# Layer 1's edge sums of a two-layer graph network, taken by quarters of the nodes instead of whole groups

## The chip, the cores and the metric

The kernel runs on one core of one Trainium2 chip. The metric is the device time of one execution in microseconds (us); three runs of the kernel before took 2122.86, 2127.27 and 2133.31 us, so its time is the median, 2127.27 us.

The engines that matter here work side by side, each through its own instructions in order: TensorE (PE in the profile, with its weight loads as PEld), VectorE (DVE), ScalarE (ACT), GpSimd (POOL), and SyncE (SP), which only issues transfers. GpSimd also issues the gathers, transfers whose source rows come from a list of indices.

## The reference

There are 3125 nodes with 768 features, and 53125 directed edges, sorted by their target node `dst`. Each edge has one of three relations. Two layers of the same attention (the first with four heads of 192 columns, the second with one head of 768) are followed by a residual sum and a layer normalisation:

```python
def rgat_conv(x, W, q, k, b, src, dst, etype, heads, out_ch, n_nodes):
    xr = jnp.einsum('nd,rdf->rnf', x, W)          # 3 relations
    oi = xr[etype, dst]
    oj = xr[etype, src]
    alpha = jax.nn.leaky_relu(oi @ q + oj @ k, 0.2)
    m = jax.ops.segment_max(alpha, dst, num_segments=n_nodes)
    e = jnp.exp(alpha - m[dst])
    z = jax.ops.segment_sum(e, dst, num_segments=n_nodes)
    a = e / (z[dst] + EPS)
    msg = (a[:, :, None] * oj.reshape(-1, heads, out_ch)).reshape(-1, heads * out_ch)
    return jax.ops.segment_sum(msg, dst, num_segments=n_nodes) + b

h = jax.nn.elu(rgat_conv(x, W1, q1, k1, b1, src, dst, edge_type, 4, 192, n))
out = rgat_conv(h, W2, q2, k2, b2, src, dst, edge_type, 1, 768, n)
x = _layernorm(x + out)
```

What the change concerns is the last `segment_sum` of layer 1: for every node, the sum over its edges of the attention weight times the source's row.

## The kernel before

**Groups and slots.** The nodes are cut into 25 groups of up to 128. The edges of a group, which lie together because they are sorted, are read as 17 slots of 128 edges (14 for the first group), 422 slots in all. One edge of a slot sits on each of the 128 partitions.

**Three phases.** `phase1` multiplies the nodes by layer 1's weights, stores the rows in a table in memory, and works out every edge's attention weight `pall` (four heads). `phase2` gathers the edges' source rows, sums them per node (layer 1's output), applies bias and ELU, and multiplies by layer 2's weights. `phase3` does layer 2's attention and sums and the normalisation. In this text `phase2` is the middle stage and `phase3` the last.

**The middle stage, slot by slot.** Slot k goes through these steps:

- `gather(k)`: GpSimd gathers 128 rows of 772 numbers into `gs[k % 9]`, one of nine tiles named `share`.
- `high(k)`: ScalarE writes H, the row times the edge's weight (four instructions, one a head) rounded to the type fp32r; VectorE or, for two slots in three, GpSimd writes `sel`, a 128x128 matrix that is 1 where an edge (row) belongs to a node (column).
- `low(k)`: VectorE writes L, what that rounding lost (four instructions).
- `sums(k)`: TensorE multiplies `sel` with H and with L, two halves each, so four matmuls of 128x386, and adds them up in `acc` in PSUM over all slots of the group.

Four early slots (k = 1, 3, 5, 7; `whole`) go another way: VectorE writes the selection matrices with the weights already in them (four of 128x128), and TensorE multiplies them with the unrounded rows, in plain fp32, which the trace shows as two matmul records for every one in the code.

When a group's sums are complete, `e_y` divides by the sum of weights and adds the bias (VectorE), `e_x` is an exponential (ScalarE), `e_h` finishes the ELU (VectorE), `e_t` transposes the result with six matmuls (TensorE), `e_s` and `e_s2` split it into two fp32r parts, and 18 pieces `d_part` of six matmuls each multiply it by layer 2's weights. `d_row` copies their sums to a row tile and stores it.

**The order is written out by hand.** The loop at the end of `phase2` counts k. Iteration k issues `gather(k)`, `sums(k - LAG)`, `low(k - LAG + 2)`, `high(k - LAG + 3)` with LAG = 8, and the events of that iteration: one `d_part` of the previous group in nearly every iteration, and the `e_` steps of a finished group over five iterations. Each engine executes its share strictly in that order.

**The last stage sums otherwise.** Because a slot's edges are sorted by node, they fall into a window of one or two quarters (32 nodes) of the group. `WINDOW` lists the quarters of each of the 17 slots, 25 pairs of slot and quarter in all, and `ROUNDS` orders the slots in seven rounds; a round's slots lie in different quarters. In `phase3` the selection matrix (`selp`) has only 32 or 64 columns and holds the weight, and each matmul has 32 output rows: the program gives it one of four column strips of the array (the profile writes 128*32 in place of 128*128). A check, `windows`, sends inputs that don't fit to a slower kernel.

Of the kernel before, what the change touches and what calls it, by code (L numbers as in the profile page):

```python
# [8 lines left out]
F32 = mybir.dt.float32  # L9
F32R = mybir.dt.float32r  # L10
# [3 lines left out]
AF = mybir.ActivationFunctionType  # L14
ALU = mybir.AluOpType
# [5 lines left out]
P = 128  # L21
# [11 lines left out]
def _index(ap):  # L33
    return bass.IndirectOffsetOnAxis(ap=ap, axis=0)
# [3 lines left out]
SL = 17  # L38
# [7 lines left out]
WINDOW = ((0,), (0,), (0,), (0, 1), (0, 1), (1,), (1,), (1, 2), (1, 2), (1, 2), (2,), (2, 3), (2, 3), (2, 3),  # L46
          (3,), (3,), (3,))

ROUNDS = ((0, 7, 15), (1, 8, 16), (2, 9, 14), (3, 11), (4, 12), (5, 13), (6, 10))
# [3 lines left out]
def kernel(  # L53
# [21 lines left out]
    R = layers[0]["W"].shape[0]  # L75
    E = src.shape[0]
    NB = (N + P - 1) // P
# [3 lines left out]
    l1, l2 = layers  # L81
    H1 = l1["H"]
    F1 = D // H1
    EP = 125
    ET = E // EP
    assert EP * ET == E and D % P == 0 and H1 == 4 and l2["H"] == 1 and R == 3
    RW = D + 4
    HW = RW // 2
    CW = F1 + 1
    LL = FRONT + E + BACK  # L90
    NK = (NB - 1) * SL + SLF
    V, S, G, T = nc.vector, nc.scalar, nc.gpsimd, nc.tensor
# [8 lines left out]
    tab1 = dram.tile([NP * R, RW], F32, name="ftab1")  # L101
# [8 lines left out]
    row = keep.tile([P, P], F32, name="frow")  # L110
# [22 lines left out]
    dl = keep.tile([P, NB, SL + 1], F32, name="fdl")  # L133
    rel = keep.tile([P, NB, SL], F32, name="rel")
    pall = keep.tile([P, NB, SL, H1], F32, name="pall")
# [131 lines left out]
    def split_parts(work, pts, w, name="t"):  # L267

        parts = []
        for i, pt in enumerate(pts):  # L270
            H, L = (work.tile([P, 2, w if name != "t" else 2 * P], F32R, name=f"{name}{s}{i}",
                              bufs=2 if name == "t" else 1) for s in "HL")
            S.copy(H[:, :, :w], pt[:, :, :w])
            V.tensor_sub(L[:, :, :w], pt[:, :, :w], H[:, :, :w].bitcast(F32))
            parts.append((H, L))
        return parts
# [168 lines left out]
    def base(b):  # L445

        return SLF + (b - 1) * SL if b else 0

    def slots(b):
        return SL if b else SLF  # L450

    def slot(k):

        return divmod(k - SLF + SL, SL) if k >= SLF else (0, k)

    ends = {base(b) + slots(b) - 1 for b in range(NB)}
    regs = {}

    def gather_rows(to, tab, b, j):

        i = ridx[:, b]
        if b in first_rows:
            i = rfirst[:, first_rows[b]]
        return G.indirect_dma_start(out=to, out_offset=None, in_=tab, in_offset=_index(i[:, j:j + 1]),  # L464
                                    bounds_check=NP * R - 1, oob_is_err=False)
# [361 lines left out]
    def phase2(work, psum, wH, wL):  # L827
        bias1 = work.tile([P, D], F32, name="fbias1", bufs=1)
        nc.sync.dma_start(bias1, l1["b"][None, :].to_broadcast([P, D]))
        last_w2 = second_weights(R - 1, wH, wL)  # L830
        gs = share
        NG = len(gs)
        rows = [work.tile([P, RW], F32, name=f"r2_{i}", bufs=1) for i in range(3)]
        for t in rows:
# [2 lines left out]
        st = {}  # L837
        blk = {}
        order = range(NB)
        ends2 = ends  # L840

        def gather(k):
            b, j = slot(k)
            gather_rows(gs[k % NG], tab1, b, j)

        def whole(k):

            return k < 8 and k % 2 == 1

        def high(k):  # L850
            b, j = slot(k)
            g = gs[k % NG]
            if whole(k):
                sel = work.tile([P, H1, P], F32, name="L", bufs=3)
                for h in range(H1):
                    V.tensor_scalar(sel[:, h], row, dl[:, b, j:j + 1], pall[:, b, j, h:h + 1],
                                    op0=ALU.is_equal, op1=ALU.mult)
                st[k] = sel
                return
            H = work.tile([P, RW], F32R, name="H", bufs=4)  # L860
            for h in range(H1):
                c = slice(h * CW, (h + 1) * CW)
                S.activation(H[:, c], g[:, c], AF.Copy, scale=pall[:, b, j, h:h + 1])  # L863
            sel = work.tile([P, P], F32R, name="sel", bufs=4)
            (V if k % 3 == 0 else G).tensor_scalar(sel, row, dl[:, b, j:j + 1], None, op0=ALU.is_equal)  # L865
            st[k] = [sel, H]

        def low(k):
            if whole(k):
                return  # L870
            b, j = slot(k)
            g = gs[k % NG]
            H = st[k][1]
            L = work.tile([P, RW], F32R, name="L", bufs=3)
            for h in range(H1):
                c = slice(h * CW, (h + 1) * CW)
                V.scalar_tensor_tensor(L[:, c], g[:, c], pall[:, b, j, h:h + 1], H[:, c].bitcast(F32),  # L877
                                       op0=ALU.mult, op1=ALU.subtract)
            st[k].append(L)

        def sums(k):
            b, j = slot(k)
            if j == 0:
                blk[b] = {"acc": psum.tile([P, 2, 512], F32, name="acc", bufs=2)}
            acc = blk[b]["acc"]
            if whole(k):
                sel = st.pop(k)
                for h in range(H1):
                    c = slice(h % 2 * CW, (h % 2 + 1) * CW)
                    T.matmul(acc[:, h // 2, c], sel[:, h], gs[k % NG][:, h * CW:(h + 1) * CW], start=False,  # L890
                             stop=(k in ends2), skip_group_check=True)
                return
            sel, H, L = st.pop(k)
            for i, a in enumerate((H, L)):
                for c in range(2):
                    T.matmul(acc[:, c, :HW], sel, a[:, c * HW:(c + 1) * HW], start=(j == 0 and i == 0),  # L896
                             stop=(k in ends2 and i == 1), skip_group_check=True)

        def e_y(b):
            s = blk[b]  # L900
# [10 lines left out]
        def e_x(b):  # L911
            s = blk[b]
            s["ey"] = work.tile([P, D], F32, name="ey", bufs=1)
            S.activation(s["ey"], s["y"], AF.Exp)
# [57 lines left out]
        def when(k, f, *a):  # L972
            ev.setdefault(k, []).append((f, a))

        LAG = 8
        first = SLF + LAG - 1
        for d, f in ((0, e_h), (1, e_t), (1, e_s), (1, e_s2)):
            when(first + d, f, order[0])
        for i, b in enumerate(order):
            e = SLF + i * SL + LAG  # L980
            if i > 0:
                for d, f in ((0, e_y), (1, e_x), (2, e_h), (3, e_t), (4, e_s), (4, e_s2)):
                    when(e + d, f, b)
            e += 6
            for m in range(6 * R):
                rc = divmod(m // 3, 2)
                k = e + m * SL // (6 * R) if i else first + 2 + m * (SL + 6) // (6 * R)
                when(k, d_part, b, *rc, m % 3)
                if m % 3 == 2:
                    when(k + 1, d_row, b, *rc)  # L990
            when(e + 2 + SL, d_q, b)
        for k in range(max(ev) + 1):
            if k < NK:
                gather(k)
            if k in (14, 19, 23, 26, 28):
                next(last_w2, None)
            if 0 <= k - LAG < NK:
                sums(k - LAG)
            if k == first:
                e_y(order[0])  # L1000
                e_x(order[0])
            if 0 <= k - LAG + 2 < NK:
                low(k - LAG + 2)
            if 0 <= k - LAG + 3 < NK:
                high(k - LAG + 3)
            for f, a in ev.get(k, []):
                f(*a)
            if k == NK + LAG:
                for b in range(len(xbs)):
                    x_load3(b)  # L1010

    def x_load3(b):

        nc.sync.dma_start(xbs[b % len(xbs)], nodes(b, xb_d))


    def phase3(work, psum):
# [3 lines left out]
        NG = 44  # L1021
        gs = work.tile([P, NG, RW], F32, name="G", bufs=1)
# [4 lines left out]
        st = {}  # L1027
# [95 lines left out]
        def a_put(b):  # L1123
            s = blk[b]
            s["p"] = work.tile([P, SL], F32, name="p2", bufs=3)
            V.tensor_copy(s["p"], s["pa"][:, 3 * P:3 * P + SL])

        def rounds(b):
            return [[j for j in r if j < slots(b)] for r in ROUNDS]

        def high(b, n):

            for j in rounds(b)[n]:
                p = blk[b]["p"][:, j:j + 1]
                lo, hi = WINDOW[j][0] * 32, WINDOW[j][-1] * 32 + 32
                sel = work.tile([P, 64], F32, name="selp", bufs=10)[:, :hi - lo]
                V.tensor_scalar(sel, row_p[:, lo:hi], dl[:, b, j:j + 1], p, op0=ALU.is_equal, op1=ALU.mult)  # L1137
                st[b, j] = sel
# [93 lines left out]
        LAG = SL + 10  # L1232
        for b in range(NB):
# [7 lines left out]
            e = base(b) + slots(b)  # L1241
# [21 lines left out]
    with tc.manual_schedule():  # L1263
        with tc.tile_pool(name="share", bufs=1) as pool:
            share = [pool.tile([P, RW], F32, name=f"share{i}") for i in range(9)]
# [3 lines left out]
            with tc.tile_pool(name="wbuf", bufs=1) as wbuf:  # L1269
                wH = wbuf.tile([P, R * DT, D + 2], F32R, name="wH")  # L1270
                wL = wbuf.tile([P, R * DT, D + 2], F32R, name="wL")
                with tc.tile_pool(name="pre", bufs=1) as pre:
                    qq = pre.tile([P, NB, H1, R], F32, name="qq")
                    with tc.tile_pool(name="work0", bufs=1) as work, tc.tile_pool(
                        name="psum0", bufs=1, space=PSUM
# [20 lines left out]
                    with tc.tile_pool(name="work1", bufs=1) as work, tc.tile_pool(  # L1296
                        name="psum1", bufs=1, space=PSUM
# [544 lines left out]
```

## Time and profile before

The profiled execution took 2122.86 us, 4.4 us under the median of the runs; its span, from the first instruction to the last, is 2121.1 us.

| stretch of the span | us | PE busy | DVE busy | ACT busy | POOL busy | granted PE clock | DMA |
|---|---|---|---|---|---|---|---|
| phase 1 and before (0 to 700) | 700 | 627.8 | 346.9 | 165.9 | 485.9 | 0.94 to 0.98 | 54 to 65% |
| start of the middle stage (700 to 740) | 40 | 29.2 | 35.3 | 27.5 | 34.1 | 0.69 | 92% |
| middle stage (740 to 1490) | 750 | 742.9 | 724.5 | 662.1 | 652.7 | 1.00 | 79 to 80% |
| its end (1490 to 1560) | 70 | 44.7 | 26.8 | 11.0 | 23.5 | 0.79 | 64% |
| last stage (1560 to 2122) | 562 | 371.5 | 330.4 | 96.0 | 407.6 | 0.71 to 0.77 | 51 to 94% |

How such views are read: the busy time of a stretch says which engines could bound it; the groups of instructions give the number, the total busy time and the mean duration of one kind of instruction; the chain of work that ended last is followed back from the end, and names at each moment the instruction that everything later hung on; the timeline lists instructions in order with the time at which they start. A duration is not the distance to the next instruction of the same engine: matmuls and VectorE instructions overlap their neighbours, so the distance from start to start is what an instruction costs an engine that is never idle.

### The profile page before, as it was taken

The page shows a single profiled execution, that of the slowest core. Times are in us where ns is not written, and L with a number is a line of the kernel's source. Part 1 is how long each engine was busy: PE and PEld are TensorE (multiplying, and loading weights), DVE is VectorE, ACT ScalarE, POOL GpSimd, SP SyncE. Part 2 cuts the span into 40 slices and gives each one's busy share as a digit, 9 for nine tenths or more (in the row PEclk, how much of TensorE's full clock was granted, in tenths as well). Part 3 has the DMA queues.
Part 4 walks back from the last instruction along what each step waited for, and adds up shares of the span by engine and source line. Part 5 has one row for each costly group of instructions (what it writes and reads, how often), then busy time and mean ns, then how long its engine had stood idle before and what let it go on. Part 6 is the DMA issues. An engine that isn't in the chain of part 4 may idle for free.

```text
span 2121.1 us, 38492 instructions
## 1 busy us (share of the span) xinstructions
PE 1816.0 (86%) x11755; PEld 1614.9 (76%) x11755; DVE 1463.8 (69%) x4299; ACT 962.4 (45%) x2331; POOL 1603.8 (76%) x1604
## 2 busy tenths in 40 slices
PE   6979998999979699999999999999856676676774
PEld 5979988999979599999999999999823343443433
DVE  6545544545543799999999999999456656656654
ACT  5411211122211588888888888888201211111111
POOL 5257777777777888888888888888177777777773
PEclk9999999999999799999999999999967777777787
DMA  6555544455538887777888778878499999999993
GB/s 184 188 146 171 194 159 148 158 187 171 171 115 266 279 260 246 232 242 242 259 247 251 246 246 251 249 244 249 162 311 325 329 338 336 328 329 317 317 321 131
DMA packets 156843, 506.10 MB, mean 239 GB/s; under 512 B 43875, under 2 KB 57069, under 8 KB 156628
## 3 DMA queue, kind: packets, MB, share of 16 engines
q0 software_dynamic: 81904, 331.52, 49.5%
q1 hardware_dynamic: 64494, 156.04, 21.2%
q10 hardware_dynamic: 10230, 15.98, 2.2%
q8 instruction: 97, 1.59, 0.3%
q14 instruction: 118, 0.97, 0.1%
HBM read 412.55 MB, written 95.69 MB: 240 GB/s over the span
## 4 chain that ended last, share of the span: by engine, by line
PE 61%; issue 11%; POOL 11%; DVE 8%; DMA 7%; ACT 1%; POOLq 0%; SPq 0%; ACTq 0%; DVEq 0%
PE po L951 21%; PE acc L896 13%; PE acc L1151 11%; POOL kt L464 8%; PE po L700 8%; DMA G<-ftab,ridx 2%; POOL G L464 2%; DMA kt<-kt,ridx 1%; PE bank L285 1%; PE pt L263 1%; DVE L L877 1%; DVE F L1108 1%; PE pt L926 1%; PE bc L1055 1%; PE po L399 1%
## 5 line engine op out<-in xcount | busy, mean ns | idle before, releaser
L863 ACT ACTIVATE H<-share,pall 128x193 fp32r<-128x193 f32 x1672 | 619.4, 447 | 83.5 <-PE acc L896 43.2
L877 DVE SCALAR_TENSOR_TENSOR L<-share,pall,H 128x193 fp32r<-128x193 f32 x1672 | 622.3, 437 | 19.9 <-issue 13.0
L951 PE MATMUL po<-wH,hT 128*128 128x386 f32 (+1 forms) x1800 | 529.7, 339 | 0.2 <-DVE hT L939 0.2
L464 POOL DMA_INDIRECT share<-ftab,ridx x374 | 421.2, 1126 | 80.5 <-DVE L L877 33.6
L464 POOL DMA_INDIRECT kt<-kt,ridx x374 | 395.0, 1056 | 114.6 <-issue 109.4
L464 POOL DMA_INDIRECT G<-ftab,ridx x374 | 379.8, 1015 | 114.0 <-issue 84.7
L700 PE MATMUL po<-wH,xT 128*128 128x384 f32 x1584 | 440.6, 348 | 10.1 <-ACT share L715 4.4
L951 PEld LDWEIGHTS po<-wH,hT 128*128 128x128 f32 x1800 | 334.4, 189 | 0.7 <-DVE hT L939 0.5
L700 PEld LDWEIGHTS po<-wH,xT 128*128 128x128 f32 x1584 | 294.0, 191 | 16.7 <-ACT share L715 6.3
L951 PE MATMUL po<-wL,hT 128*128 128x386 f32 (+1 forms) x900 | 304.9, 339 | 0.0
L1151 PE MATMUL acc<-G,selp 128*32 128x386 f32 x2488 | 299.3, 578 | 3.6 <-DVE selp L1137 2.1
L700 PE MATMUL po<-wL,xT 128*128 128x384 f32 x792 | 270.0, 341 | 0.0
L1151 PEld LDWEIGHTS acc<-G,selp 128*32 128x32 f32 x2488 | 185.9, 127 | 79.6 <-issue 46.6
L896 PE MATMUL acc<-H,sel 128*128 128x386 f32 x836 | 223.8, 349 | 10.8 <-POOL sel L865 9.7
L865 POOL TENSOR_SCALAR sel<-frow,fdl 128x128 fp32r<-128x128 f32 x278 | 215.9, 777 | 15.4 <-PE acc L896 4.7
L896 PE MATMUL acc<-L,sel 128*128 128x386 f32 x836 | 218.3, 343 | 0.0
L715 ACT COPY share<-po 128x384 f32<-128x384 f32 x144 | 67.7, 477 | 276.3 <-PE po L700 273.0
L1202 ACT ACT_TABLE_LOAD x24 | 30.8, 1283 | 356.2 <-DVE sd L1198 356.2
L951 PEld LDWEIGHTS po<-wL,hT 128*128 128x128 f32 x900 | 169.7, 189 | 0.0
L896 PEld LDWEIGHTS acc<-H,sel 128*128 128x128 f32 x836 | 150.8, 190 | 17.5 <-POOL sel L865 15.8
L896 PEld LDWEIGHTS acc<-L,sel 128*128 128x128 f32 x836 | 155.4, 192 | 0.2 <-DVE L L877 0.2
L1061 DVE TENSOR_SCALAR sT<-bc,cols 128x512 bf16<-128x512 f32 (+1 forms) x125 | 83.4, 667 | 99.0 <-PE bc L1055 98.9
(248 smaller groups left out, 2140.9 us busy)
## 6 DMA issues: line engine op xcount, KB each, us to landing
ftab<-share SPq DMA_DIRECT2D x75, 386.0 KB
ftab<-r SPq DMA_DIRECT2D x75, 386.0 KB
share<-in_L_gnn_W_dram SPq DMA_DIRECT2D x36, 384.0 KB
w_d<-w2hl SPq DMA_DIRECT2D x18, 768.0 KB
sT<-dr_d SPq DMA_DIRECT2D x25, 544.0 KB
share<-in_x_dram SPq DMA_DIRECT2D x25, 384.0 KB
xb_d<-share SPq DMA_DIRECT2D x25, 384.0 KB
xr<-in_x_dram SPq DMA_DIRECT2D x23, 384.0 KB
```

Of the source, the lines that this page charges most:

```text
L263: T.transpose(pt[:, f, c * P:(c + 1) * P], a[:, (2 * i + f) * P:(2 * i + f + 1) * P], ident)
L464: return G.indirect_dma_start(out=to, out_offset=None, in_=tab, in_offset=_index(i[:, j:j + 1]), bounds_check=NP * R - 1, oob_is_err=False)
L700: m = T.matmul(po[:, :HALF], xT[:, s, t, :], w[:, i, sl], start=(n == 0), stop=(n == 3 * DT - 1))
L715: S.copy(to, po[:, :HALF].rearrange("p (h f) -> p h f", h=2))
L863: S.activation(H[:, c], g[:, c], AF.Copy, scale=pall[:, b, j, h:h + 1])
L865: (V if k % 3 == 0 else G).tensor_scalar(sel, row, dl[:, b, j:j + 1], None, op0=ALU.is_equal)
L877: V.scalar_tensor_tensor(L[:, c], g[:, c], pall[:, b, j, h:h + 1], H[:, c].bitcast(F32), op0=ALU.mult, op1=ALU.subtract)
L896: T.matmul(acc[:, c, :HW], sel, a[:, c * HW:(c + 1) * HW], start=(j == 0 and i == 0), stop=(k in ends2 and i == 1), skip_group_check=True)
L951: T.matmul(po[:, :wd], hT[:, k, t, :], w[:, r * DT + t, sl], start=(t == 0 and n == 0), stop=(t == DT - 1 and n == 2))
L1061: V.tensor_scalar(s["sT"][:, 4 * i * P:4 * i * P + n], bc[:, :n], cols[:, b:b + 1], None, op0=ALU.is_equal)
L1151: T.matmul(acc[32 * t:32 * t + 32, c, :HW], st[b, j][:, 32 * (t - WINDOW[j][0]):][:, :32], gs[:, (base(b) + j) % NG, c * HW:(c + 1) * HW], ...
L1202: S.activation(sd, sd, AF.Sqrt)
```

## The change

In the middle stage, H, L, the 128x128 `sel` and the `whole` path go. VectorE writes, for each slot, four selection matrices with the weights in them (one a head), 32 or 64 columns wide, 9 slots deep. TensorE multiplies them in plain fp32 with the gathered rows, a quarter and a head at a time (32 output rows, 193 columns). The slots of a group are taken in the order of `ROUNDS` (`in_turn`), and the sums are issued two rounds at a time: after the sixth, the eleventh, the fifteenth and the last slot of a group (four batches). The ring of gathered rows grows from 9 tiles to 14. LAG is 5 in place of 8, and the steps of the first group move a little. The function `rounds` moves out of `phase3`; the last stage is otherwise the same, instruction for instruction.

```diff
-        gs = share
+        gs = share + [work.tile([P, RW], F32, name=f"g{i}", bufs=1) for i in range(5)]
...
+        def in_turn(k):
+            b, i = slot(k)
+            return b, [j for r in rounds(b) for j in r][i]
 
         def gather(k):
-            b, j = slot(k)
-            gather_rows(gs[k % NG], tab1, b, j)
+            gather_rows(gs[k % NG], tab1, *in_turn(k))
...
         def high(k):
-            H = work.tile([P, RW], F32R, name="H", bufs=4)
-            for h in range(H1):
-                c = slice(h * CW, (h + 1) * CW)
-                S.activation(H[:, c], g[:, c], AF.Copy, scale=pall[:, b, j, h:h + 1])
-            sel = work.tile([P, P], F32R, name="sel", bufs=4)
-            (V if k % 3 == 0 else G).tensor_scalar(sel, row, dl[:, b, j:j + 1], None, op0=ALU.is_equal)
+            b, j = in_turn(k)
+            lo, hi = WINDOW[j][0] * 32, WINDOW[j][-1] * 32 + 32
+            sel = work.tile([P, H1, 64], F32, name="selp", bufs=9)
+            for h in range(H1):
+                V.tensor_scalar(sel[:, h, :hi - lo], row[:, lo:hi], dl[:, b, j:j + 1], pall[:, b, j, h:h + 1],
+                                op0=ALU.is_equal, op1=ALU.mult)
+            st[b, j] = sel, gs[k % NG]
...
-        def low(k):
-                V.scalar_tensor_tensor(L[:, c], g[:, c], pall[:, b, j, h:h + 1], H[:, c].bitcast(F32),
-                                       op0=ALU.mult, op1=ALU.subtract)
...
         def sums(k):
-            for i, a in enumerate((H, L)):
-                for c in range(2):
-                    T.matmul(acc[:, c, :HW], sel, a[:, c * HW:(c + 1) * HW], ...)
+            b, j = in_turn(k)
+            n = [i for i, r in enumerate(rounds(b)) if r[-1] == j]
+            if not n or n[0] % 2 == 0 and n[0] < len(ROUNDS) - 1:
+                return
...
+            o = [(i, t) for r in rounds(b) for i in r for t in WINDOW[i]]
+            for m, h in ((m, h) for m in range(n[0] // 2 * 2, n[0] + 1) for h in range(H1)):
+                c = slice(h % 2 * CW, (h % 2 + 1) * CW)
+                for i, t in o:
+                    if i not in rounds(b)[m]:
+                        continue
+                    u = [x for x, y in o if y == t]
+                    sel, g = st[b, i]
+                    T.matmul(acc[32 * t:32 * t + 32, h // 2, c], sel[:, h, 32 * (t - WINDOW[i][0]):][:, :32],
+                             g[:, h * CW:(h + 1) * CW], start=(i == u[0] and h % 2 == 0), stop=(i == u[-1]),
+                             skip_group_check=True)
...
-        LAG = 8
+        LAG = 5
         first = SLF + LAG - 1
-        for d, f in ((0, e_h), (1, e_t), (1, e_s), (1, e_s2)):
+        for d, f in ((0, e_h), (3, e_t), (3, e_s), (3, e_s2)):
             when(first + d, f, order[0])
...
-                low(k - LAG + 2)
-            if 0 <= k - LAG + 3 < NK:
-                high(k - LAG + 3)
+                high(k - LAG + 2)
```

## The prediction

> **What bounds the kernel now.** The change lies in the middle stage only, so I first read the busy times by stretch, then the chain of waits inside the stage, then the groups of its instructions, and last the timeline of the last stage, which already sums in the new way.
>
> Two stretches, the middle stage and the last (columns: length; PE, PEld, DVE, ACT, POOL busy with counts; granted clock, DMA share, GB/s):
>
> ```profile
> 1000.00:1250.00 250.00, 249.42 (x1425) 248.02 (x1424) 242.83 (x713) 222.26 (x597) 217.53 (x225) 1.00 0.80 248
> 1800.00:2050.00 250.00, 168.26 (x1391) 97.96 (x1390) 152.95 (x452) 45.44 (x57) 192.40 (x190) 0.76 0.92 322
> ```
>
> TensorE is busy for 249.4 of 250 us at full clock in the middle stage; VectorE, at 97%, is close behind, so taking work from VectorE, ScalarE or GpSimd alone gains little. The chain of waits there (start us, us, what) is TensorE and next to nothing else:
>
> ```profile
> 1003.08 2.13 PE po L951 x12
> 1005.21 0.71 PE acc L896 x4
> 1005.92 1.06 PE po L951 x6
> ```
>
> A slot's sums (L896, four matmuls) cost TensorE 0.71 us, a piece of the product with the second layer's weights (L951, six) 1.06 us. The first term is what changes. In the groups (count, then busy us, mean ns) the other engines' share of it, and the last stage's `selp`:
>
> ```profile
> L863 ACT ACTIVATE H<-share,pall 128x193 fp32r<-128x193 f32 x1672 | 619.4, 447 | 83.5 <-PE acc L896 43.2
> L877 DVE SCALAR_TENSOR_TENSOR L<-share,pall,H 128x193 fp32r<-128x193 f32 x1672 | 622.3, 437 | 19.9 <-issue 13.0
> L1137 DVE TENSOR_SCALAR selp<-row_p,fdl,p 128x32 f32<-128x32 f32 x222 | 65.4, 304 | 42.8 <-PE acc L1151 41.9
> L1137 DVE TENSOR_SCALAR selp<-row_p,fdl,p 128x64 f32<-128x64 f32 x200 | 63.3, 337 | 5.5 <-PE acc L1151 5.5
> L865 POOL TENSOR_SCALAR sel<-frow,fdl 128x128 fp32r<-128x128 f32 x278 | 215.9, 777 | 15.4 <-PE acc L896 4.7
> ```
>
> And the new kind of sum, in the last stage's timeline (start us, us), with its durations (min/median/max ns) below:
>
> ```profile
> 1703.91 0.39 PE L1055 MATMUL bc<-d,one 1*128 1x512 bf16 x1
> 1704.23 2.80 PE L1151 MATMUL acc<-G,selp 128*32 128x386 f32 x28
> 1704.58 0.13 PEld L1151 LDWEIGHTS acc<-G,selp 128*32 128x32 f32 x4 [0.19 <-issue]
> 1704.90 0.13 PEld L1151 LDWEIGHTS acc<-G,selp 128*32 128x32 f32 x4 [0.20 <-issue]
> 1706.96 0.39 PE L1055 MATMUL bc<-d,one 1*128 1x512 bf16 x1
> 1708.70 1.01 POOL L464 DMA_INDIRECT G<-ftab,ridx  x1 [0.30 <-issue]
> 1710.02 1.01 POOL L464 DMA_INDIRECT G<-ftab,ridx  x1 [0.30 <-issue]
> ```
>
> ```profile
> L1151 PE MATMUL acc<-G,selp x2488: 484/488/856, 1560.4 to 2107.1; 128*32 128x386 f32 x192
> ```
>
> The same view of the start of the middle stage: selections and fp32 sums of the `whole` path, the first group's last sum, the first product piece; below, from the chain there, a gather that lands late:
>
> ```profile
> 711.08 1.11 DVE L856 TENSOR_SCALAR L<-frow,fdl,pall 128x128 f32<-128x128 f32 x4
> 714.80 1.48 PE L890 MATMUL acc<-share,L 128*128 128x193 f32 x8
> 728.33 0.85 PE L896 MATMUL acc<-L,sel 128*128 128x386 f32 x2
> 734.63 0.40 PE L951 MATMUL po<-wH,hT 128*128 128x386 f32 x1
> ```
>
> ```profile
> 713.40 8.60 DMA share<-ftab,rfirst
> ```
>
> The weight loads come four at a time, 0.325 us apart (1704.58, 1704.90): up to four quarters' matmuls start together, and the next four after 0.325 us. A start of four thus costs what one 386-column fp32 record costs. For 193 columns L890 gives it: eight in 1.48 us, the last of which takes 0.33, so (1.48 - 0.33) / 7 = 0.165 us from start to start, half of 0.325, with 128 weight columns loaded behind each.
>
> **The sums on TensorE.** Removed: 17 x 0.71 = 12.07 us a group. Added: seven rounds x four heads x two records = 56 starts of up to four, 56 x 0.165 = 9.24 us a group. The L1151 count confirms two records a matmul (2488 for 1244 in the code).
>
> The Trainium skill's page TensorE: Matmul & The Clock Gate, section "Part 3: Packing small matmuls", speaks against this: four packed row tiles gave 3.07 times the speed there, three column tiles 2.38. By that page a group's sums would take an estimated 9.24 x 4 / 3.07 = 12.0 us, and nothing would be saved. The row here has four starting in the time of one, so 9.24 stays.
>
> **The switch between whole and quarter matmuls.** Each of the four batches a group stands between L951 pieces, so TensorE changes shape 8 times a group. The trace prices it at L1055, a whole-width matmul among quarters. A 386-column fp32 record takes 0.488 and is followed after 0.325, so 0.163 of a duration is tail; L1055 (0.39) should be followed after 0.22, and is after 0.315 (1703.91 to 1704.225): 0.09 in. The last quarters start at 1704.23 + 2.80 - 0.49 = 1706.54, the whole one at 1706.96, after 0.42 in place of 0.325: 0.10 out. The second start of a batch comes 0.02 late, and the first 128-column weight load after it isn't hidden: 0.10, what a sums' first matmul loses after a wait in the middle stage (two in 0.62 us against 0.52). Together 0.31 a batch. Ends: 0.20 (the two drains alone) and 0.70 (each switch waits for the whole tail, 0.163, and a 128-column load, 0.19). I take 0.31, the nearest row.
>
> The Trainium skill's page TensorEngine Tiling (Array Packing), section "Key Properties", says that a change of the tiling mode drains the engine. It names no price; the trace agrees that there is one, 0.09 to 0.10 a switch.
>
> **After the first product piece.** Before, from 734.63 to the stage's last matmul at 1527.5, 407 slots' sums stand on the chain: 407 x 0.71 = 289.0 us. After: 24 groups x 9.24 = 221.8, and 96 batches x 0.31 = 29.8. The gain is 37.4 us. The 450 pieces (477 us) and 25 transposes stay.
>
> **What covers the rest, and what if not.** VectorE loses L877 (a group's 68) and gets 68 `selp`: 36 of 32 columns, 32 of 64. At L1137's mean durations, 36 x 0.304 + 32 x 0.337 = 21.7 us, plus some 6 for a group's other VectorE work (four `y` 1.6, `e_h` 1.5, the hT part 0.95, ten small ones 1.9), is 27.7 of about 30.3 us: covered even so. The distance from start to start is less (L856, 128 columns: (1.11 - 0.34) / 3 = 0.26), which makes some 23 us. ScalarE loses H and is nearly idle. GpSimd loses `sel` (216 us); back to back, gathers go 1.31 us apart in the last stage, 17 x 1.31 = 22 us a group. DMA, at 0.80, has the same bytes in 5% less time: 0.84, under the 0.92 that it reaches later. These four edits cost nothing on the path.
>
> VectorE's new wait (for a free `selp`, nine deep) is for a batch that lies at least two iterations back, so `e_y` and `e_h` queued behind it aren't held. A batch needs up to six gathers at once, but with 14 tiles each is issued 9 or more iterations (some 15 us) ahead.
>
> **The transposes.** After a group's last batch TensorE has five pieces, 5 x 1.06 + 0.2 = 5.5 us, before `e_t`. Meanwhile: 0.24 to the first VectorE instruction, 0.15 + 0.18 + four `y` at 0.37 (L877, of the same size, goes eight in 2.98 us) with gaps, 2.0; two slots' `selp` 1.7 (ScalarE's exponential, 0.85, lies beside them); `e_h` 0.56 + 0.97; 5.5 us in all. It just fits: before, slot sums between the pieces gave more room. I take 0; the other end, with durations in place of pitches, is 6.3, so 0.8 a group, 19 us.
>
> **The start.** Before, the first group's last sum ends at 729.2, then 5.4 us follow until the first piece. After, it hangs on the 14th gather: issued from 695.76 every 1.31 us, so at 712.8; one issued at 713.40 landed after 8.6 us, so 721.5; then eight starts at half clock, 8 x 0.33 = 2.6, and 724.1 or a little later. I take 4.5 us gained, between 0 and 10 (landing in 3 us).
>
> **Sum.** 37.4 + 4.5 = 42 us. The profiled execution (2122.9) would become 2081; the median of the runs, 4.4 us above it, 2127.3 - 42 = 2085. The last stage keeps its order and only starts earlier.
>
> **Rivals.**
> - Same time: the switch costs its upper bound, 0.70 a batch: 96 x 0.39 = 37 us lost, 2122. For it: no row shows a switch from an fp32r product. Against: both drains seen are 0.1.
> - VectorE is late at every `e_t`: 2085 + 19 = 2104. For it: the margin is nil. Against: today TensorE waits there four times, 0.4 us at most.
> - Slower: the quarter loads no longer hide. A set of four takes 0.13 us; behind 0.325 that leaves 0.19, behind 0.165 only 0.03. If a start became load plus stream, 0.29, it would cost 24 x 56 x 0.125 = 168 us, 2253. Each 0.01 us costs 13 us, so it decides from 0.165 + 0.031, about 0.196 a start. Against: L890 hides 128-column loads behind the same 193 columns.
>
> **How the numbers follow.** A difference under 0.5% (10.6 us) can't be told from no change here. Forecast 2085: 0.66; `e_t` late, 2104: 0.16; the switch at its bound: 0.09; loads not hidden: 0.09. So faster 0.82, same 0.09, slower 0.09. The range goes from switches at 0.20 and a start gain of 10 (2085 - 10.6 - 5.5 = 2069, and a few us more for small waits that go, 2064) to halfway between the second case and the third, 2116.
>
> **What would show it.** In the changed kernel's middle stage: starts of four 0.165 us apart; 0.1 us extra on each side of a batch; PE still over 95% busy at clock 1.00; ACT under 20%; no wait of `pt` for `ey` over 0.5 us; the first piece near 730, the stage's last matmul near 1485. Wrong if starts lie 0.2 us or more apart, if gaps at batches exceed 0.35, if VectorE's idle time falls to nothing, or if the granted clock drops below 1.00.

## The result, and the profile after it

The changed kernel takes 2072.75 us (median of 4 runs, 2070.48 to 2076.27), the kernel before 2130.29 beside it: a ratio of 0.973, 95% interval 0.969 to 0.977. The forecast was 2085, with a range of 2064 to 2116. The profiled execution took 2070.48 us with a span of 2068.7, which is 52.4 us less span than before, where the forecast had 42.

The stretch 1000 to 1250 of the middle stage, as shown of before (columns: length; PE, PEld, DVE, ACT, POOL busy with counts; granted clock, DMA share, GB/s):

```profile
1000.00:1250.00 250.00, 250.00 (x2586) 216.97 (x2588) 169.14 (x708) 38.93 (x68) 137.94 (x138) 1.00 0.78 261
```

TensorE is still the bound, now without a gap. VectorE fell from 243 to 169 us, ScalarE from 222 to 39, GpSimd from 218 to 138. The chain of waits shows one group from its transposes (L909) to the next ones:

```profile
1005.25 0.66 PE pt L909 x6
1005.90 1.05 PE po L934 x6
1006.95 2.77 PE acc L878 x64
1009.72 6.52 PE po L934 x36
1016.24 2.76 PE acc L878 x64
1019.00 4.42 PE po L934 x24
1023.42 2.76 PE acc L878 x56
1026.19 2.33 PE po L934 x12
1028.52 1.44 PE acc L878 x16
1029.96 5.49 PE po L934 x30
1035.44 0.65 PE pt L909 x6
```

Four batches (`acc`, 200 records) stand between 108 matmuls of the product, and 1035.44 - 1005.25 = 30.19 us is a group. Taken over all groups between 794 and 1458, it is 30.22. The edges of one batch, in the timeline (start us, us):

```profile
1006.62 0.33 PE L934 MATMUL po<-wH,hT 128*128 128x384 f32 x1
1006.88 0.35 PE L878 MATMUL acc<-g,selp 128*32 128x193 f32 x1
1006.89 0.37 PE L878 MATMUL acc<-share,selp 128*32 128x193 f32 x3
1007.07 0.33 PE L878 MATMUL acc<-g,selp 128*32 128x193 f32 x1
1007.23 0.33 PE L878 MATMUL acc<-g,selp 128*32 128x193 f32 x1
...
1009.65 0.44 PE L934 MATMUL po<-wH,hT 128*128 128x384 f32 x1
1009.93 0.34 PE L934 MATMUL po<-wL,hT 128*128 128x384 f32 x1
1010.10 0.51 PE L934 MATMUL po<-wH,hT 128*128 128x384 f32 x2
```

Four quarters start within 0.01 us of each other, and the next four 0.165 later. Whole matmuls follow each other after 0.177. From the last whole one to the first quarters it is 0.26, and behind the batch the second whole one comes 0.28 after the first. Over 89 batches the medians are: in 0.268, last quarters to first whole 0.255, first whole to second 0.281. The batch loses 0.09 on the way in, 0.03 at its second start, 0.09 on the way out and 0.10 at the first whole matmul, 0.31 in all. The `acc` pieces of the chain hide most of it, since two of these parts are put down to `po`. A batch's price is read from starts, not from the chain's pieces.

By stage the 52.4 us are:

| | before | after | less |
|---|---|---|---|
| start to the first product piece | 734.6 | 733.4 | 1.2 |
| first piece to the stage's last matmul | 792.9 | 746.9 | 46.0 |
| from there to the end | 593.6 | 588.4 | 5.2 |

### The profile page after: what moved, and what is told of

Its sections match the earlier page's. It is cut to its first block, busy times and chain, and to the rows that moved or that the text cites. A ratio compares the mean times of both kernels' runs of the same rounds, so it can differ in the third digit from the quotient of the medians.

```text
span 2068.7 us, 41981 instructions
## 1 busy us (share of the span) xinstructions
PE 1770.4 (86%) x15027; PEld 1477.3 (71%) x15027; DVE 1195.9 (58%) x4159; ACT 375.8 (18%) x659; POOL 1328.1 (64%) x1326
## 4 chain that ended last, share of the span: by engine, by line
PE 61%; issue 12%; POOL 11%; DMA 8%; DVE 7%; ACT 1%; POOLq 0%; SPq 0%; DVEq 0%; ACTq 0%
PE po L934 23%; PE acc L1129 12%; PE acc L878 11%; POOL kt L466 9%; PE po L702 8%; DMA wL<-w_d 1%; POOL G L466 1%; PE bank L285 1%; PE pt L263 1%; DMA kt<-kt,ridx 1%; DVE F L1089 1%; PE bc L1036 1%; DVE stats L1172 1%; PE po L399 1%; PE pt L909 1%
## 5 line engine op out<-in xcount | busy, mean ns | idle before, releaser
L857 DVE TENSOR_SCALAR selp<-frow,fdl,pall 128x32 f32<-128x32 f32 (+1 forms) x1688 | 380.4, 318 | 0.2 <-PE acc L878 0.2
L466 POOL DMA_INDIRECT share<-ftab,ridx x239 | 238.9, 999 | 177.7 <-PE acc L878 132.9
L466 POOL DMA_INDIRECT g<-ftab,ridx x135 | 134.9, 999 | 113.3 <-PE acc L878 88.0
L878 PE MATMUL acc<-share,selp 128*32 128x193 f32 x3208 | 190.6, 331 | 5.1 <-DMA share<-ftab,rfirst 4.1
L942 ACT COPY r<-po 128x386 f32<-128x386 f32 (+1 forms) x150 | 72.3, 482 | 604.7 <-PE po L934 603.1
L878 PEld LDWEIGHTS acc<-share,selp 128*32 128x32 f32 x3208 | 122.8, 111 | 51.1 <-issue 15.4
L702 PEld LDWEIGHTS po<-wL,xT 128*128 128x128 f32 x792 | 152.3, 192 | 0.0
L1115 DVE TENSOR_SCALAR selp<-row_p,fdl,p 128x32 f32<-128x32 f32 (+1 forms) x422 | 110.7, 320 | 47.7 <-PE acc L1129 46.8
L1036 PE MATMUL bc<-d,one 1*128 1x512 bf16 (+1 forms) x125 | 48.6, 388 | 85.0 <-DVE sT L1042 82.3
L878 PE MATMUL acc<-g,selp 128*32 128x193 f32 x1768 | 118.6, 329 | 1.9 <-DMA g<-ftab,rfirst 1.9
```

The source lines that it names most:

```text
L702: m = T.matmul(po[:, :HALF], xT[:, s, t, :], w[:, i, sl], start=(n == 0), stop=(n == 3 * DT - 1))
L857: V.tensor_scalar(sel[:, h, :hi - lo], row[:, lo:hi], dl[:, b, j:j + 1], pall[:, b, j, h:h + 1], op0=ALU.is_equal, op1=ALU.mult)
L878: T.matmul(acc[32 * t:32 * t + 32, h // 2, c], sel[:, h, 32 * (t - WINDOW[i][0]):][:, :32], g[:, h * CW:(h + 1) * CW], start=(i == u[0] an ...
L942: S.copy(o[:, c * HW:c * HW + wd], po[:, :wd])
L1036: T.matmul(bc[:, :n], one, s["d"][:, 4 * i * P:4 * i * P + n], start=True, stop=True)
```

## Experiments

Theory: the gain is TensorE's own time, 12.07 us of whole sums a group against 56 starts of 0.165 and four batches of 0.31. Against it stand that packing isn't what makes the sums cheap, that a batch costs something else, and that the work taken off the other engines pays.

Runs are compared within their set, each on one chip and beside the kernel before. The first set (the first four kernels below) ran on a chip on which the kernel before took 2547 us, and every kernel reached its middle stage some 285 us later. The changed kernel itself was not run on that chip. There, only what lies on TensorE without waits is read.

**Seven batches a group.**

```
+FLUSH = (0, 1, 2, 3, 4, 5, 6)
...
-            if not n or n[0] % 2 == 0 and n[0] < len(ROUNDS) - 1:
+            if not n or n[0] not in FLUSH:
                 return
-            if n[0] < 2:
+            first_m = max([f + 1 for f in FLUSH if f < n[0]], default=0)
+            if first_m == 0:
...
-            for m, h in ((m, h) for m in range(n[0] // 2 * 2, n[0] + 1) for h in range(H1)):
+            for m, h in ((m, h) for m in range(first_m, n[0] + 1) for h in range(H1)):
```

> The changed kernel with seven batches of sums a group (one round each) in place of four: 75 more batches in all, the same matmuls. Theory (each batch costs TensorE 0.31 us: 0.09 in, 0.03 at the second start, 0.09 out, 0.10 at the first whole matmul after): 75 x 0.31 = 23 us more than the changed kernel's 2073, so 2096, and a group of the middle stage 0.93 us longer, 31.15 in place of 30.22. Rival (the chain of waits is right, in which four batches are 0.5 us longer than their starts, 0.12 each): 9 us more, 2082, a group 30.6. Rival 2 (with smaller batches, gather tiles come free earlier and something else shortens): 2073 or less.

2521 us, ratio 0.990 (0.986 to 0.994). No matmul of the stage waited, and a group takes 31.20 us, as two transposes in the chain show:

```profile
1301.10 0.65 PE pt L912 x6
1332.31 0.66 PE pt L912 x6
```

The time is 0.98 more than 30.22 for three batches more: 0.33 a batch. The price from the starts holds, the 0.12 from the chain's pieces falls.

**Three batches, and two.** The same edit with batches after other rounds, for three

```
-FLUSH = (0, 1, 2, 3, 4, 5, 6)
+FLUSH = (1, 3, 6)
```

and for two

```
-FLUSH = (0, 1, 2, 3, 4, 5, 6)
+FLUSH = (2, 6)
...
-            sel = work.tile([P, H1, 64], F32, name="selp", bufs=9)
+            sel = work.tile([P, H1, 64], F32, name="selp", bufs=12)
```

> The changed kernel with three batches a group (rounds 0-1, 2-3 and 4-6; the last holds six slots) in place of four. Theory (0.31 a batch): 25 x 0.31 = 8 us less than 2073, so 2065, a group 29.91 us. Rival (0.12 a batch): 2070. Rival 2 (the last batch now waits for its last slot with more work in it, and the eighth of the sums that stood apart was free): 2073.

> The changed kernel with two batches a group (rounds 0-2, nine slots; rounds 3-6, eight slots) and twelve selp buffers in place of nine. Theory (0.31 a batch): 50 x 0.31 = 15.5 us less, 2057, a group 29.60 us. Rival (nine tiles come free at once and GpSimd issues the gathers 1.31 us apart, so that they land late and TensorE waits for gathered rows): 2073 or more, with waits of the sums for gathers in the middle stage. A first group summed in two batches starts its first batch later, which can cost up to 3 us once.

2656 us (ratio 1.044) and 2693 us (1.058), with groups of 35 to 42 us. The three-batch kernel's timeline, TensorE and then ScalarE:

```profile
1393.86 0.51 PE L937 MATMUL po<-wH,hT 128*128 128x384 f32 x2
...
1397.05 0.34 PE L937 MATMUL po<-wH,hT 128*128 128x386 f32 x1
1399.62 0.51 PE L937 MATMUL po<-wH,hT 128*128 128x384 f32 x1 [2.23 <-issue]
```

```profile
1399.09 0.48 ACT L945 COPY r<-po 128x384 f32<-128x384 f32 x1 [9.12 <-remote]
1400.65 0.48 ACT L945 COPY r<-po 128x386 f32<-128x386 f32 x1 [1.08 <-remote]
```

Three pieces of 384 columns end with the matmul that starts at 1393.86, the next three, of 386, with the one at 1397.05; a matmul here takes 0.34 us. ScalarE had been idle for 9 us, yet it starts their copies only at 1399.09 and 1400.65, 4.9 and 3.3 us after those ends (`remote`: the profile doesn't name what released it). Over the stage's copies before which ScalarE stood idle, the median is 3.2 us and the longest 5.6; the changed kernel's copies follow after 0.08. TensorE then waits for the first of the two copies to free `po`. The signal came late, not the work. Whether this belongs to the chip or to fewer batches was open, so the two-batch kernel ran again beside the changed one.

> The changed kernel once more, as a yardstick for the others of this set, since the set before ran on a chip on which the kernel before itself took 2547 us: there, TensorE's signals to other engines came up to 3 us after the matmul that sends them (in the first set's traces), which they don't in the first two traces. If that belongs to the chip and not to the kernels, the kernel before is again near 2130 us on another chip, the changed one near 0.973 of it, and signals follow the matmul's end by 0.01 to 0.03 us in the middle stage. If this set sees slow signals too, the ratio is open: between 0.96 (the gain of 1.7 us a group of 32) and 1.05 (the changed kernel hangs more on the signals of a few large batches).

> The same kernel as two_batches (rounds 0-2 and 3-6 as batches, twelve selp buffers), beside the changed kernel on one chip. Theory (0.31 a batch, nothing else): 50 x 0.31 = 15.5 us less than the changed kernel, ratio to the kernel before about 0.966, a group of the middle stage 29.60 us in place of 30.22. Rival (its gathers come in bursts of nine and eight and land late, which is what made it slow in the set before, not the chip): waits of TensorE in the middle stage also without slow signals, a group over 31 us, slower than the changed kernel.

On this chip the kernel before took 2133 us, the changed one 2079.7 (0.975, 0.970 to 0.980), two batches 2058.1 (0.965, 0.960 to 0.970), and the copies followed after 0.08 us in the median, 0.4 at most, in both. So larger batches alone don't bring the late signals. Two batches take 29.66 us a group against 30.21, 0.55 less, where 0.62 was expected. Of the 21 us less span, 12 are 22 groups at 0.55, and 5.5 lie in the first two groups, where the changed kernel waited 2.8 us for a part of the second layer's weights (`wL`) to arrive: they took 36.1 and 31.0 us here, 32.4 and 30.2 in its first profile. The rest is in the start and the last stage. The three-batch kernel wasn't repeated.

**The order within a batch.**

```
-            for m, h in ((m, h) for m in range(n[0] // 2 * 2, n[0] + 1) for h in range(H1)):
-                c = slice(h % 2 * CW, (h % 2 + 1) * CW)
-                for i, t in o:
-                    if i not in rounds(b)[m]:
-                        continue
+            for m in range(n[0] // 2 * 2, n[0] + 1):
+                for i, t, h in ((i, t, h) for i, t in o if i in rounds(b)[m] for h in range(H1)):
+                    c = slice(h % 2 * CW, (h % 2 + 1) * CW)
```

> The changed kernel with the order of a batch's matmuls turned: all four heads of one quarter after each other, then the next quarter, so that successive matmuls fall on the same 32 columns; the same matmuls and sums. Theory (what makes the sums cheap is that four quarters start together; two matmuls on the same quarter follow each other at 0.165 us a record): a round takes about 4 x 8 x 0.165 = 5.3 us less some overlap where the quarter changes, in place of 1.32; up to 28 us a group more, so some 60 us a group, near 2700 us in all. Rival (TensorE runs matmuls of different quarters beside each other whatever their order, as long as the weights are loaded ahead): 2073. Rival 2 (a matmul with a quarter of the columns is itself a quarter of the cost, and nothing runs beside anything): 2073.

2751 us (one execution), beside 2547 for the kernel before. The chain:

```profile
1306.47 6.24 PE acc L876 x64
1312.71 6.55 PE po L932 x36
1319.26 6.24 PE acc L876 x64
```

The same 64 records take 6.24 us in place of 2.77, and a group 40.6, where some 60 were expected; both rivals, with 2073, fall. So what makes the sums cheap is four quarters side by side, and the order of issue decides it. The cost is less than one after another (64 x 0.165 = 10.6): as the start times read, mostly two quarters run beside each other, the last records of one with the first of the next.

**The removed work put back on ScalarE and GpSimd.**

```
+            for h in range(H1):
+                S.activation(junkH[:, h % 2 * CW:(h % 2 + 1) * CW], bias1[:, :CW], AF.Copy, scale=pall[:, b, j, h:h + 1])
+            if k % 3:
+                G.tensor_scalar(junks, row, dl[:, b, j:j + 1], None, op0=ALU.is_equal)
```

> The changed kernel, with the work that the change took off ScalarE and GpSimd put back beside it, on tiles that nobody reads: four 193-column copies with a scale on ScalarE for each slot, and a 128x128 selection on GpSimd for two slots of three. Nothing on TensorE or VectorE changes. Theory (the gain is TensorE's time alone; ScalarE and GpSimd were off the path): within 6 us of the changed kernel (under 0.3%), ScalarE above 80% busy and GpSimd near 85% in the middle stage. Rival (the kernel before lost time where TensorE waited for GpSimd's selections queued behind gathers, some 8 us of the 46, and GpSimd that is late with a gather costs the same): 5 to 15 us more. Rival 2 (freeing the two engines is a large part of the gain): 20 us or more back.

2094.3 us (ratio 0.981, 0.976 to 0.986), 14.5 more than the changed kernel, with ScalarE 90% and GpSimd 84% busy. TensorE's waits from 735 to 1440 (us, times, longest):

```profile
PE pt L915 <- DVE ey L908: 9.0, 14, 6.1
PE po L940 <- ACT hT L922: 3.0, 1, 3.0
```

The theory's 6 us falls, and so does the first rival's mechanism, though its size fits: no wait of the sums for a gather. The time goes to the transposes. The exponential queues behind the fills on ScalarE, `e_h` comes late (the longest wait, 6.1, is the first group's), and a group takes 30.60 in place of 30.21. Of the 14.6 us of span, 4.8 lie between the first sums and the first piece, where the same chain has no cover and ScalarE can't start its fills before 713.35, when the bias row that they read has landed. 5.1 lie between the first piece and the stage's last matmul (22 groups at 0.39 are 8.6, but the changed kernel's first two were slow in its execution), 1.0 before the first sums, and 3.7 in the last stage, which has none of the added work.

**More VectorE work.**

```
+            V.scalar_tensor_tensor(junkL[:, :CW], bias1[:, :CW], pall[:, b, j, 0:1], bias1[:, CW:2 * CW],
+                                   op0=ALU.mult, op1=ALU.subtract)
```

> The changed kernel, with one more 193-column VectorE instruction for each slot (a product and a difference like the removed L, on tiles that nobody reads): 17 x 0.437 = 7.4 us of VectorE more a group, so that it is busy for about 92% of a group's 30.2 us in place of 67%. Theory (VectorE's free third is not what the time hangs on): within 10 us of the changed kernel. Rival (what is queued behind the fill is late: the chain from a group's last sum through y and ey to the transposes, which had 5.5 us of cover with nothing over by the forecast's working): each group's transposes 1 us or more late, 25 us or more in all.

2096.5 us (0.982, 0.977 to 0.987), 16.8 more, with VectorE only 206 of 250 us busy, 83%: the fills follow each other faster than their duration says. The chain:

```profile
1050.88 0.89 DVE selp L858 x4
1051.76 0.27 DVE junkL L861
1052.03 0.89 DVE selp L858 x4
1052.92 0.33 DVE junkL L861
1053.25 0.48 DVE ey L904
...
1053.75 0.97 DVE ey L905
...
1054.86 0.84 PE pt L912 x6
```

Two fills, 0.60 us, stand between the last sum and the transposes, which now wait in each of 23 groups; a group takes 30.80, 0.59 more. So the rival's mechanism holds, at about half its size: a third of VectorE was free, yet these two instructions on this chain lengthened every group. Where TensorE waits, the transposes start 0.15 us after `e_h`; in the changed kernel 0.27 after it. It had 0.12 us to spare.

The 16.8 us overstate the fills' work, since they brought a wait of their own. They read the bias row, and at the start VectorE waits for it:

```profile
721.13 0.42 DVE L861 SCALAR_TENSOR_TENSOR junkL<-fbias,pall 128x193 fp32r<-128x193 f32 x1 [8.57 <-DMA fbias<-in_L_gnn_b_dram]
```

Of the 19.5 us of span, 10.8 lie between the first piece and the stage's last matmul, 7.5 between the first sums and the first piece, where this wait stands, and 2.2 before; the last stage is 1.0 shorter. Whether the theory's 10 us would have held without that wait is not shown.

**Fewer gather tiles.**

```
-        gs = share + [work.tile([P, RW], F32, name=f"g{i}", bufs=1) for i in range(5)]
+        gs = share + [work.tile([P, RW], F32, name=f"g{i}", bufs=1) for i in range(2)]
```

> The changed kernel with eleven gather tiles in place of fourteen (two new ones in place of five). A tile comes free when its batch is done; with eleven, a gather is issued at least six slots, 10.7 us, before the batch that needs it is due, in place of nine slots, 16 us. Theory (the gathers have room to spare: in the changed kernel GpSimd itself waits for free tiles about a third of the time): within 6 us of the changed kernel, a group at 30.2 us; the start 0 to 5 us later, since fewer gathers are under way there. Rival (the five tiles are what lets large batches work): waits of the sums for gathers in every group, 1 us or more each, 25 us or more in all.

2070.8 us (0.971, 0.968 to 0.973), a group 30.16. Waits of TensorE's weight loads for gathers in the whole stage:

```profile
PEld acc L878 <- DMA share<-ftab,rfirst: 0.4, 1, 0.4
PEld acc L878 <- DMA share<-ftab,ridx: 0.2, 1, 0.2
```

Three of the five new tiles cover nothing with four batches.

**What the kernel before lost to its helpers.** Groups of before between 800 and 1440 took 31.7 to 32.4 us, but two took 34.0 and 33.7, and the first 38.1. Its waits in the stage, matmuls and weight loads:

```profile
PE acc L896 <- POOL sel L865: 5.7, 6, 2.3
```

```profile
PEld acc L896 <- POOL sel L865: 9.8, 13, 2.7
```

```
-            sel = work.tile([P, P], F32R, name="sel", bufs=4)
-            (V if k % 3 == 0 else G).tensor_scalar(sel, row, dl[:, b, j:j + 1], None, op0=ALU.is_equal)
-            st[k] = [sel, H]
+            st[k] = [picked.pop(k), H]
...
+            sel = picked[k] = work.tile([P, P], F32R, name="sel", bufs=7)    # two iterations earlier
```

> The kernel before, with its 128x128 selections (sel) made two iterations earlier and seven buffers for them in place of four; nothing else moves. In the kernel before's trace, TensorE waited for these selections 17 times in the middle stage (5.4 us in the waits of its matmuls, 9.2 us in those of its weight loads), three groups lasted 34 to 38 us in place of 31.9, and the forecast, which counts every slot's sums at 0.71 us, has none of this. Theory (these waits are GpSimd's selections queued behind gathers that wait for a free tile, and are the 8 us that the middle stage gained beyond the forecast): 5 to 9 us less, ratio near 0.997, no wait for sel, groups at 31.9 us. Rival (the gathered rows themselves are late there, and the wait only takes another name): no change, ratio 1.000.

2132.3 us, ratio 0.9986 (0.9964 to 1.0008): no gain that can be told from none. TensorE's waits for `sel` are gone, and others stand there:

```profile
PE pt L933 <- DVE ey L926: 15.7, 15, 3.3
PE acc L903 <- DVE L L884: 1.8, 6, 0.5
```

The theory falls. The rival's number holds, but TensorE's waits are for `ey` and L, not for gathers; behind them ScalarE waited 38.0 us for gathered rows (7.9 in the kernel before), so late gathers are not excluded by this run. VectorE stayed 94 to 96% busy, and what is made earlier there may make something else late. So both helpers were relieved:

```
-            for h in range(H1):
-                c = slice(h * CW, (h + 1) * CW)
+            for h in (0, 2):
+                c = slice(h * CW, (h + 2) * CW)
                 V.scalar_tensor_tensor(L[:, c], g[:, c], pall[:, b, j, h:h + 1], H[:, c].bitcast(F32),
...
-            (V if k % 3 == 0 else G).tensor_scalar(sel, row, dl[:, b, j:j + 1], None, op0=ALU.is_equal)
+            V.tensor_scalar(sel, row, dl[:, b, j:j + 1], None, op0=ALU.is_equal)
```

> The kernel before with its helpers relieved and TensorE's work unchanged: L is made by two 386-column VectorE instructions a slot in place of four of 193 (so heads 1 and 3 get their neighbour's weight in L; the output is not the reference's), and all selections (sel) are made on VectorE, none on GpSimd. Worked out from the kernel before's rows: VectorE 17 x (4 x 0.437 - 2 x 0.62) = 8.6 us a group less, 11 x 0.31 = 3.4 more, so from 97% to about 80% busy; GpSimd is left with gathers. Theory (the 8 us that the middle stage gained beyond TensorE's own saving are stalls that come from VectorE and GpSimd being full: when sel came earlier, the wait only moved to the transposes): groups at 31.9 us throughout, no waits of the sums or transposes over 0.5 us, 6 to 10 us less, ratio 0.996. Rival (the stalls come from gathers that land late, in DMA): ratio 1.000 and groups of 33 to 38 us remain.

2111.1 us, ratio 0.991 (0.989 to 0.994): 19.8 us less, about twice the 6 to 10 that were expected.

```profile
PE pt L926 <- DVE ey L919: 0.8, 1, 0.8
```

That is its only wait of a matmul in the stage, and ScalarE no longer waits for gathered rows. Groups take 31.69 to 31.85 (the first 34.7), VectorE is 88% busy, and the stage from the first piece to the last matmul takes 782.0 us against 792.9. So 10.9 us of the kernel before were stalls that went with its full helpers, with TensorE's work unchanged; which of the two helpers matters more is not separated. The two profiles' spans differ by 16.1 us, of which 4.9 lie in the last stage, whose code is the same.

Three groups of the kernel before hold 7.5 of the 10.9 us. In each, the wait for `sel` follows a gather that kept GpSimd for 3.0 to 3.3 us, where the median is 1.1:

```profile
877.42 4.04 DVE L877 SCALAR_TENSOR_TENSOR L<-share,pall,H 128x193 fp32r<-128x193 f32 x12
879.41 3.01 POOL L464 DMA_INDIRECT share<-ftab,ridx  x1 [0.30 <-PE acc L896]
882.46 1.00 POOL L865 TENSOR_SCALAR sel<-frow,fdl 128x128 fp32r<-128x128 f32 x1
883.51 0.62 PE L896 MATMUL acc<-H,sel 128*128 128x386 f32 x2 [1.13 <-POOL sel L865]
```

Each of these gathers lies beside a run of VectorE instructions without a break, nearly all of them L. With its helpers relieved, no gather of the stage takes over 1.5 us, in the changed kernel none over 1.1. That such a run holds a gather up fits these rows, but was not tested by itself.

From the relieved kernel to the changed one a group falls from 31.78 to 30.22, 1.56 us, which is TensorE's own saving.

**A faster version.** Two batches, with the exponential and `e_h` one iteration earlier:

```
-                for d, f in ((0, e_y), (1, e_x), (2, e_h), (3, e_t), (4, e_s), (4, e_s2)):
+                for d, f in ((0, e_y), (0, e_x), (1, e_h), (3, e_t), (4, e_s), (4, e_s2)):
```

> two_batches with the exponential (e_x) and the step after it (e_h) one iteration earlier for every group but the first, so that one slot's selections fewer (0.9 us) stand in VectorE's queue between a group's last sum and its transposes. In two_batches_again, TensorE lost about 0.2 us at the transposes of 20 groups, and a group took 29.66 us. Theory (that loss is e_h coming just too late): a group 29.5 us, 4 us less than two_batches in all, ratio to the kernel before 0.963. Rival (the 0.2 us belongs to the transposes' own weight loads): 29.66 us as before.

2055.7 us, ratio 0.964 (0.961 to 0.967), the lowest of all; it was not run on the first set's chip, where two batches were slower than the kernel before. The chain:

```profile
999.48 0.65 PE pt L912 x6
...
1005.39 4.08 PE acc L881 x96
...
1018.15 5.39 PE acc L881 x104
...
1029.04 0.66 PE pt L912 x6
```

A group takes 29.57 us and no wait of a matmul is left. Against the 29.66 of two batches alone (whose time can't be told from this one's) that is 0.09, half of what was expected of the earlier `e_h`. Against the changed kernel it is 0.64 for two batches, 0.32 each.

## Why the forecast held, point by point

The time lies in the range, and the mechanism of the main term is right, but the gain was underestimated. In the spans of the two profiles, 52.4 us were gained where 42 were forecast: 10.9 of stalls that had no term and 5.2 in the last stage came on top, and 3.3 at the start (1.2 in place of 4.5) and 2.3 of the middle stage's own 37.4 stayed away.

- **Sums, 12.07 to 9.24 us a group.** Right. Starts of four lie 0.165 us apart. Less four batches of 0.31, the forecast had 1.59 a group; calm groups give 1.56. Four quarters run in the time of one here; the Trainium skill's page TensorE: Matmul & The Clock Gate, section "Part 3: Packing small matmuls", with 3.07 for four row tiles and 2.38 for three column tiles, is not what these traces show for 193 fp32 columns.
- **Switch, 0.31 a batch.** Right, part by part, and by three kernels: 0.33 (seven batches against four), 0.32 (two, early), 0.28 (two, where about 0.1 a group went to the transposes).
- **"Taking work from VectorE, ScalarE or GpSimd alone gains little."** Too strong, and the largest miss: the sum counted each old slot at 0.71 us and had no term for TensorE's waits in the kernel before. Relieving the helpers alone is worth 10.9 us in the middle stage; with the 35.1 from there to the changed kernel that is the 46.0 that were gained. The row was there: two groups of 34 us, and waits for `sel` of 5.7 us before matmuls (9.8 before weight loads, in part the same time).
- **The transposes, 0.** Right, and the working "it just fits" too: 0.12 us to spare. Of the two kernels that put work on that chain, one lost 0.39 us a group and the other 0.59.
- **The start, 4.5 us.** Wrong: 1.2. The step that failed is "the first group's last sum ends at 729.2, then 5.4 us follow". VectorE shows that the sum ending at 729.2 is the second group's. Before:

```profile
727.22 0.15 DVE L903 TENSOR_SCALAR rz<-acc 128x4 f32<-128x4 f32 x1
```

  and after:

```profile
726.43 0.16 DVE L886 TENSOR_SCALAR rz<-acc 128x4 f32<-128x4 f32 x1 [7.06 <-PE acc L878]
```

  The group's sums end 0.8 us earlier, not 5; from there to the first piece it is 7.4 us before and 7.0 after, the same chain. Unchanged code before it ended 2.1 us later in this execution, which hid as much.
- **VectorE at 75 to 90%, DMA at 0.84.** It was 68% and 0.78. Selections of 64 columns start 0.22 us apart, where the forecast's two ends had 0.26 and 0.34. Neither engine sets the time.
- **Last stage, 0.** It is 5.2 us shorter. It was 588 to 595 us long in the profiles of the kernels whose last stage is the same, so it may be scatter; this wasn't tested.
- **The rivals.** The switch stayed far from 0.70, the quarter loads stay hidden, and the transposes were not late. The range's upper end is a slip: halfway between 2104 and 2122 is 2113, not 2116. The result is far from both.

## What to carry to other kernels

Price a packed matmul by the distance from start to start, and its batch by the gaps at both edges, then group the work into as few batches as the buffers allow: each batch cost 0.32 us here. Check that on the chip at hand, since on the first set's chip three and two batches were slower than the kernel before. Keep the strips of one round next to each other in the issue order. When an engine is 97% busy beside a full TensorE, look for stalls by the length of single periods, not by its share; and when it has a third free, look for the one chain that has no slack before putting anything on it.

## What was not expected of the hardware

- TensorE ran matmuls of neighbouring quarters beside each other only as far as their order allowed: 2.77 us for 64 records with four quarters in turn, 6.24 with four heads of a quarter in turn.
- On the first set's chip, ScalarE's copies (those before which it stood idle) followed TensorE's pieces after 3.2 us in the median with three batches; with two, 46 of 149 came after more than 0.5 us (up to 5.8). With seven batches, and with the turned order, it was 0.09 in the median and over 0.5 in 1 and 4 of 150; on the other chips it was 0.08 in the changed and the two-batch kernel. Why was not found.
- A group's six transposes cost TensorE 0.75 us from the last piece's last start to the next piece's first start. With an idle gap of 0.38 before them it is 1.32, 0.57 more: a wait also lays bare the last 0.16 us of the matmul before it, which the next one covers otherwise. The chain's 0.66 and 0.84 don't show this.
- Three fewer gather tiles, 16 us of lead cut to 11, cost nothing, though a gather at the start of the stage took over 8 us to land.
